# A hand-written order for the first batch's entry, an early activation table, filler matmuls, and later LoRA loads

## The chip, the cores and the metric

The kernel runs on one core of one Trainium2 chip. The metric is the device time of one execution in microseconds (us), taken as the median of several runs. Engines are named as in the profile: PE multiplies matrices into PSUM, DVE is the vector engine, ACT the scalar engine, POOL the third elementwise engine, SP issues most DMA transfers. [...]

## The reference

Two batches of 1024 tokens, 2048 features each. The first step normalises x per token, quantises it and a 2048 x 2048 context to 8 bits and adds their product to x; the second adds a 2048 x 2048 linear layer with a gated and a shared LoRA.

```python
def fake_quant(x, scale, zp):
    q = jnp.clip(jnp.round(x / s + z), 0.0, 255.0)
    return (q - z) * s
x = x + matmul(fake_quant(layernorm(x)), fake_quant(ctx))
h = layernorm(x)
x = x + h @ kernel + bias + (h @ A_eff.T) @ B_eff.T + (h @ A_shared.T) @ B_shared.T
```

## The kernel before

**Tiles.** A batch is 8 token tiles m of 128 rows (`prep_x`), two to a group g (4 groups, `y[g]`). The context is cut into 4 blocks n of 512 columns; a block comes in 8 loads of 256 rows (0.5 MB each). A *pair* (n, g) is the product of block n with group g: 2 x 16 matmuls of 128x128 by 128x512 (`xattn_pair`, line 367).

**One context load** (`quantise`): ACT scales and rounds it to int16 (line 318), DVE clips it, takes 128 off and writes bf16 (line 321). Three int16 buffers (`q2b`) lie between the two. Ten buffers (`lit`) take the loads; a load is issued when the one that used its buffer before has been rounded.

**One token tile** (`prep_x`): four `bn_stats` on DVE (283), their sum (257), the root on ACT (261), five small DVE steps to scale and offset (263 to 291), the row written as bytes by DVE (297), then for each half of the row: bytes less 128 to bf16 on ACT (302), 8 transposes on PE (307) and a copy out of PSUM by DVE (308). The sums give `r_s` (311, 312), the token's correction.

**One pair.** ACT writes column correction plus token correction into PSUM (365), PE adds the 16 products, DVE scales the result into y (381) and takes the statistics for the second normalisation (383). The column correction (`column_term`) is 16 narrow matmuls (337), a DVE copy (347), one matmul (349) and a DVE step (352). The very first pair has no column correction yet and gets both corrections from DVE afterwards (379). Pairs take three PSUM tiles in turn.

**Blocks 2 and 3** use the buffers of blocks 0 and 1, so block 2 can be written only when the last pair of block 0 has been multiplied. Between their loads come the LoRA A steps (`lora_a_step`: 394, 406, 414, 417), which need the gate matrix `gmat`, built at the start (236 to 248, 713).

**What sets the order.** A planner orders each engine's instructions by its own costs and priorities; `tc.high_priority` moves some ahead, `issue_after` keeps some back. None of them is written out by hand in the first batch.

**After the four blocks** come the second normalisation (439 to 450), `lora_ax` (459, copied out by ACT at 467), and the linear layer as a two-level fast product (630, 648), with `Delta` adding the LoRA part: each step loads a piece of `bd` and of the bias on ACT's queue (488, 489). In the second batch the entry is mixed into the first batch's linear layer.

Of the kernel before, what the change touches and what calls it, by code (L numbers as in the profile page):

```python
# [10 lines left out]
F32 = mybir.dt.float32  # L11
BF16 = mybir.dt.bfloat16
U8 = mybir.dt.uint8
# [53 lines left out]
def tile_quant_xattn_then_lora_ffn(  # L67
# [119 lines left out]


    sc = const.tile([P, 4], F32, tag="sc", name="sc")
    for i, s in enumerate((x1_scale, x1_zp, x2_scale, x2_zp)):  # L190
        (nc.sync, nc.scalar)[i % 2].dma_start(out=sc[:, i : i + 1], in_=s.partition_broadcast(P))
    load_x(0, 0)
    ahead[0] = 2
    load_next()
    load_x(0, 1)
    ahead[0] = 9
    load_next()
    load_x(0, 2)
    load_x(0, 3)

# [28 lines left out]
    for tag in ("acc0", "acc1", "delta"):  # L229
# [3 lines left out]


    m_ad = const.tile([P, NL], F32, tag="m_ad", name="m_ad")
    nc.vector.tensor_reduce(m_ad, ident.rearrange("p (n r) -> p n r", r=RC), AX.X, ALU.add)
    m_rk = const.tile([P, RC], F32, tag="m_rk", name="m_rk")
    nc.vector.tensor_reduce(m_rk, ident.rearrange("p (n r) -> p r n", r=RC), AX.X, ALU.add)
    gate_b = const.tile([P, GB, NL], F32, tag="gate_b", name="gate_b")
    nc.scalar.dma_start(  # L240
        out=gate_b.rearrange("p b n -> p (b n)"),
        in_=gate.rearrange("b n -> (b n)").partition_broadcast(P),
    )
    gval = const.tile([P, GB], F32, tag="gval", name="gval")
    nc.vector.tensor_tensor(gate_b, gate_b, m_ad.unsqueeze(1).to_broadcast([P, GB, NL]), ALU.mult)
    for b in range(B):
        for i in range(2):
            nc.vector.tensor_reduce(
                gval[:, ds(b * GPB + i * 2, 2)], gate_b[:, b * GPB + i : (b + 1) * GPB : 2, :], AX.X, ALU.add
            )  # L250

    def norm_stats(stats, name):
# [4 lines left out]
        nc.vector.tensor_scalar_add(ve, mv[:, 1:2], EPS)  # L259
        sd = small.tile([P, 1], F32, tag="sd", name=f"sd_{name}")  # L260
        nc.scalar.activation(sd, ve, AF.Sqrt)
        r0 = small.tile([P, 1], F32, tag="r0", name=f"r0_{name}")
        nc.vector.reciprocal(r0, sd)

        t = small.tile([P, 1], F32, tag="nt", name=f"nt_{name}")
        nc.vector.scalar_tensor_tensor(t, ve, r0, r0, ALU.mult, ALU.mult)
        nc.vector.tensor_scalar(t, t, -0.5, 1.5, ALU.mult, ALU.add)
        rstd = small.tile([P, 1], F32, tag="rstd", name=f"rstd_{name}")
        nc.vector.tensor_mul(rstd, r0, t)
        return mv[:, 0:1], rstd  # L270
# [5 lines left out]

    def prep_x(b, m, c1T, wk):

        nm = f"{b}_{m}"
        g, tok = m // MG, ds((m % MG) * P, P)  # L280
        ym = y[g][:, m % MG, :]
        for n in range(NN):
            nc.vector.bn_stats(st1[:, m, n, :], ym[:, ds(n * NB, NB)])  # L283
        with tc.high_priority() if b == 0 else nullcontext():
            mean, rstd = norm_stats(st1[:, m], f"a{nm}")

            k = small.tile([P, 1], F32, tag="kx", name=f"kx_{nm}")
            nc.vector.tensor_mul(k, rstd, inv1)
            o = small.tile([P, 1], F32, tag="ox", name=f"ox_{nm}")
            nc.vector.tensor_mul(o, mean, k)  # L290
            nc.vector.tensor_sub(o, z1, o)

            wf = flat(wk)
            q8 = wf[:, ds((m % 2) * (D // 4), D // 4)].bitcast(U8)
            qh = wf[:, D // 2 : D].bitcast(BF16)
            if b == 0:
                nc.vector.tensor_scalar(q8, ym, k, o, ALU.mult, ALU.add)
            else:
                nc.scalar.activation(q8, ym, AF.Identity, bias=o, scale=k)
        rsum = small.tile([P, 2], F32, tag="rsum", name=f"rsum_{nm}")  # L300
        for h in range(2):
            nc.scalar.activation(  # L302
# [3 lines left out]
            for kt in range(KH):  # L306
                nc.tensor.transpose(pt[:, kt, :], qh[:, ds(h * H + kt * P, P)], ident_h)  # L307
# [620 lines left out]
```

## Time and profile before

| what | value |
|---|---|
| median of 3 runs (lowest, highest) | 1118.43 us (1118.21, 1119.88) |
| the profiled execution, whole | 1118.22 us |
| its span of instructions | 1116.4 us |
| PE busy | 1070.9 us, 96% of the span |
| DVE, ACT, POOL busy | 752.5, 244.8, 262.2 us |
| PE's granted clock, mean of the execution | 0.994 |
| HBM traffic | 235 GB/s over the span |

Durations come from this one execution. Its whole time is 1.8 us more than its span, and 0.2 us less than the median. In a line of the timeline the columns are start, duration, engine, line, operation, output<-inputs, shape and count, and in brackets how long the engine sat idle before and what ended it. In a line of the stretches: the stretch, its length, busy time and number of instructions for each engine, the granted PE clock (1.00 is full), the busy share of the DMA engines and GB/s.

### The profile page before, as it was taken

To read this page: it belongs to the slowest core of one execution; us is meant where nothing else is said; L and a number is where in the kernel's file an instruction comes from. 1 tells how busy PE (TensorE), PEld (TensorE's weight loads), DVE (VectorE), ACT (ScalarE), POOL (GpSimd) and SP (SyncE) were. 2 spreads that over 40 slices of the span, in tenths; PEclk is the share of its full clock that TensorE was granted. 3 is DMA by queue.
4 is the path that set the end of the run, shared out by engine and by line. 5 is a ranking of instruction groups with operands and counts; after the bars stand their busy time and mean duration, and the time that the engine had idled before them with its cause. 6 is when DMAs were issued, how large, how long until landed. Compare 5 with 4: busy or idle time off the path is not lost.

```text
span 1116.4 us, 10654 instructions
## 1 busy us (share of the span) xinstructions
PE 1070.9 (96%) x3930; PEld 494.4 (44%) x3930; DVE 752.5 (67%) x979; ACT 244.8 (22%) x348; POOL 262.2 (23%) x106
## 2 busy tenths in 40 slices
PE   2699999999999999999999999999999999999998
PEld 1244435554444444444444433455444444444443
DVE  5895557566696677568768554766569686865851
ACT  4754414220000000001375651232000000000000
POOL 0000000234345413434000000022435343152600
PEclk9799999999999999999999999999999999999999
DMA  7982936887679746599866094588768874748511
GB/s 302 394 248 74 284 137 228 285 296 254 242 269 382 280 168 237 174 335 312 289 186 210 13 289 137 195 299 313 254 227 288 307 259 177 254 146 318 207 38 56
DMA packets 120772, 261.35 MB, mean 234 GB/s; under 512 B 11920, under 2 KB 16144, under 8 KB 119568
## 3 DMA queue, kind: packets, MB, share of 16 engines
q1 hardware_dynamic: 99264, 218.65, 56.7%
q10 hardware_dynamic: 21456, 42.02, 11.0%
q8 instruction: 31, 0.51, 0.2%
q14 instruction: 21, 0.17, 0.0%
HBM read 224.99 MB, written 37.75 MB: 235 GB/s over the span
## 4 chain that ended last, share of the span: by engine, by line
PE 81%; DVE 8%; DMA 6%; ACT 4%; issue 1%; SPq 0%; ACTq 0%; DVEq 0%
PE fu L630 33%; PE fv L630 17%; PE pa L367 12%; PE fw L630 9%; PE pl L502 3%; PE ptz L443 2%; DMA lit<-in_ctx_dram 2%; DVE st L283 2%; DMA zs<-lit 1%; PE px L459 1%; ACT big L302 1%; DMA lit<-in_lora_a_dram 1%; PE pg_b L394 1%; ACT q2b L318 1%; DMA bd<-q2b 1%
## 5 line engine op out<-in xcount | busy, mean ns | idle before, releaser
L630 PE MATMUL fu<-big,lit 128*128 128x512 f32 x896 | 395.3, 593 | 0.0
L579 POOL TENSOR_TENSOR lit<-lit,lit 128x1024 f32<-128x1024 f32 x56 | 162.4, 2908 | 523.9 <-DMA zs<-lit 202.0
L630 PEld LDWEIGHTS fu<-big,lit 128*128 128x128 f32 x896 | 168.7, 190 | 206.2 <-issue 204.9
L367 PE MATMUL pa<-big,big 128*128 128x512 bf16 x1024 | 239.4, 384 | 6.8 <-DVE big L321 3.9
L630 PE MATMUL fv<-big,lit 128*128 128x512 f32 x448 | 198.1, 594 | 0.0
L570 POOL TENSOR_TENSOR lit<-lit,lit 128x1024 f32<-128x1024 f32 x40 | 99.3, 2482 | 292.8 <-DMA lit<-zs 252.0
L579 DVE TENSOR_TENSOR big<-big,big 128x2048 f32<-128x2048 f32 x56 | 159.0, 2843 | 5.7 <-PE ptz L443 5.1
L367 PEld LDWEIGHTS <-big 128*128 128x128 bf16 x1024 | 97.7, 99 | 142.1 <-issue 39.8
L648 DVE TENSOR_TENSOR y<-y,fu 128x1024 f32<-128x1024 f32 (+1 forms) x98 | 113.7, 1194 | 66.1 <-PE fu L630 65.8
L630 PEld LDWEIGHTS fv<-big,lit 128*128 128x128 f32 x448 | 84.3, 190 | 105.0 <-issue 104.7
L648 DVE TENSOR_TENSOR y<-y,fv 128x1024 f32<-128x1024 f32 x48 | 56.8, 1218 | 89.2 <-PE fv L630 89.2
L318 ACT ACTIVATE q2b<-lit,sc,inv 128x1024 int16<-128x1024 f32 x64 | 76.6, 1230 | 156.9 <-DMA lit<-in_ctx_dram 140.5
L570 DVE TENSOR_TENSOR big<-big,big 128x2048 f32<-128x2048 f32 x40 | 101.2, 2529 | 10.9 <-DMA big<-in_w_dram 7.1
L630 PE MATMUL fw<-big,lit 128*128 128x512 f32 x224 | 99.1, 592 | 0.0
L381 DVE SCALAR_TENSOR_TENSOR y<-pa,k_s,y 128x1024 f32<-128x1024 f32 x32 | 41.0, 1281 | 62.2 <-PE pa L367 62.2
L491 ACT COPY pl<-bias 128x1024 f32<-128x1024 f32 x16 | 16.3, 1018 | 293.8 <-DVE y L513 281.2
L365 ACT ACTIVATE pa<-bp,r_s 128x512 f32<-128x512 f32 x62 | 41.4, 684 | 114.0 <-PE pa L367 65.3
L630 PEld LDWEIGHTS fw<-big,lit 128*128 128x128 f32 x224 | 42.2, 190 | 51.8 <-issue 51.8
L648 DVE TENSOR_TENSOR y<-y,fw 128x1024 f32<-128x1024 f32 x24 | 28.4, 1217 | 50.5 <-PE fw L630 50.5
L307 PE MATMUL pt<-ident_h,big 128*128 128x128 bf16 x256 | 20.4, 231 | 26.6 <-ACT big L302 26.2
L283 DVE BATCH_NORM_STATS2 st<-y 128x6 f32<-128x512 f32 x64 | 41.9, 681 | 2.2 <-DMA y<-in_x_dram 2.2
L321 DVE TENSOR_SCALAR big<-q2b 128x1024 bf16<-128x1024 int16 x64 | 27.4, 438 | 22.3 <-ACT q2b L318 18.5
(84 smaller groups left out, 625.2 us busy)
## 6 DMA issues: line engine op xcount, KB each, us to landing
big<-in_w_dram SPq DMA_DIRECT2D x96, 1024.0 KB
lit<-zs SPq DMA_DIRECT2D x88, 512.0 KB
lit<-in_ctx_dram SPq DMA_DIRECT2D x64, 512.0 KB
out_dram<-y ACTq DMA_DIRECT2D x30, 512.0 KB
zs<-lit ACTq DMA_DIRECT2D x24, 512.0 KB
y<-in_x_dram SPq DMA_DIRECT2D x8, 1024.0 KB
lit<-in_lora_a_dram SPq DMA_DIRECT2D x32, 256.0 KB
lit<-in_lora_bt_dram SPq DMA_DIRECT2D x32, 256.0 KB
```

Of the source, the lines that this page charges most:

```text
L283: nc.vector.bn_stats(st1[:, m, n, :], ym[:, ds(n * NB, NB)])
L318: nc.scalar.activation(qi, t, AF.Relu, bias=z2, scale=inv2)
L321: nc.vector.tensor_scalar(c2[r // 4][:, ds(2 * (r % 4), 2), :], qi, QMAX, CENTRE, ALU.min, ALU.subtract)
L365: nc.scalar.activation(pa[:, j, :], colt[n], AF.Identity, bias=r_s[:, m : m + 1])
L367: nc.tensor.matmul(pa[:, j, :], c1T[g][:, k, ds(j * P, P)], c2[k // 8][:, k % 8, :], start=(first_product and k == 0), stop=(k == KT - 1), ...
L381: summed = nc.vector.scalar_tensor_tensor(yp, pa, s12, yp, ALU.mult, ALU.add)
L443: nc.tensor.transpose(pt[:, k, :], t[:, ds((4 * u + k) * P, P)], ident)
L502: nc.tensor.matmul(pl[j][i][:, half], axT[rows, pr, ds(j * P, P)], bt[rows, half], start=False, stop=True, skip_group_check=True,)
L570: line(eng.tensor_tensor(got[0], got[0], got[1], ALU.add if terms[1][2] > 0 else ALU.subtract))
L579: line(eng.tensor_tensor(out_t, at[p], at[q], op))
L630: nc.tensor.matmul(ps[:, m, :], at[:, k, ds(m * P, P)], bt[:, k, :], start=(opens and k == 0), stop=(ends and k == KQ - 1), skip_group_che ...
L648: line(nc.vector.tensor_tensor(yp, yp, chains[chain][:, js, :], ALU.add if sign > 0 else ALU.subtract))
```

## The change

For the first batch only, a function `entry` writes out every step of blocks 0 and 1 and of all eight token tiles; `in_order` ties the instructions of DVE, ACT and PE to that order. The work is the same but for this:

- A root of a constant (`warm`) runs on ACT at the start, so the table for the root is loaded there.
- The first context load comes alone ahead of the second token tile.
- The gate values are loaded and reduced after the entry and not at the start.
- Scale and offset take five DVE steps with none for the plain reciprocal deviation (two fewer for a row written by DVE, one fewer for one by ACT), and `r_s` takes one instruction for two. This holds in both batches.
- In tiles 4, 5 and 6 the row of bytes is written by ACT, not DVE; in tiles 4 to 7 the second half's copy out of PSUM is ACT's.
- The pairs (0, 0) and (1, 0) begin without corrections and get them from DVE (`late`).
- Filler matmuls (`keep_busy`): 8 behind the first root, 14 behind the first column correction. Nothing reads them.
- The `bn_stats` of the eight pairs come after the entry; their DVE scaling stays in it but for the last two.
- Work on block 2 is kept back behind the entry's last ACT instruction in the planned order; before, three of its roundings ran in between.
- In both batches the loads of `bd` and bias in `Delta` are kept back behind the copy at the end of the first `lora_ax`.

```diff
+    last_of = {}
+    @contextmanager
+    def in_order(*engines):
+        traced = nc.cur_bb.bb.instructions
+        last = traced[-1]
+        yield
+        start = next(k for k in reversed(range(len(traced))) if traced[k] is last) + 1
+        for i in list(traced[start:]):
+            if i.engine in engines:
+                if i.engine in last_of:
+                    tc.add_manual_dep(
+                        i,
+                        last_of[i.engine].name,
+                        mybir.DependencyInfo(mybir.DependencyClass.NoSync, mybir.DependencyReason.DATA),
+                        reason="in_order",
+                    )
+                last_of[i.engine] = i
     sc = const.tile([P, 4], F32, tag="sc", name="sc")
     for i, s in enumerate((x1_scale, x1_zp, x2_scale, x2_zp)):
         (nc.sync, nc.scalar)[i % 2].dma_start(out=sc[:, i : i + 1], in_=s.partition_broadcast(P))
+    warm = const.tile([P, 1], F32, tag="warm", name="warm")
+    nc.gpsimd.memset(warm, 1.0)
+    nc.scalar.activation(warm, warm, AF.Sqrt)
     load_x(0, 0)
-    ahead[0] = 2
+    ahead[0] = 1
     load_next()
     load_x(0, 1)
-    ahead[0] = 9
+    ahead[0] = 8
     load_next()
     load_x(0, 2)
     load_x(0, 3)
+    ahead[0] = 9
...
+    def gate_values():
...
+    class XTile:
+        def __init__(self, b, m, c1T, wk):
...
+            self.on_vector = b == 0 and m not in (4, 5, 6)
+            self.q8 = wf[:, ds((m % 2) * (D // 4), D // 4)].bitcast(U8)
...
+        def stats(self, *ns):
+            for n in ns:
+                nc.vector.bn_stats(st1[:, self.m, n, :], self.y[:, ds(n * NB, NB)])
+        def root(self):
+            self.root_d()
+            self.root_a()
+        def root_d(self):
+            self.mean, self.ve = variance(st1[:, self.m], f"a{self.nm}")
+        def root_a(self):
+            self.sd = root_of(self.ve, f"a{self.nm}")
+        def factors(self):
+            r0, t = end_norm(self.ve, self.sd, f"a{self.nm}")
+            self.k = small.tile([P, 1], F32, tag="kx", name=f"kx_{self.nm}")
+            nc.vector.scalar_tensor_tensor(self.k, r0, t, inv1, ALU.mult, ALU.mult)
+            self.o = small.tile([P, 1], F32, tag="ox", name=f"ox_{self.nm}")
+            if self.on_vector:
+                nc.vector.scalar_tensor_tensor(self.o, self.mean, self.k, z1, ALU.mult, ALU.subtract)
+            else:
+                nc.vector.tensor_mul(self.o, self.mean, self.k)
+                nc.vector.tensor_sub(self.o, z1, self.o)
+        def row(self):
+            if self.on_vector:
+                nc.vector.tensor_scalar(self.q8, self.y, self.k, self.o, ALU.mult, ALU.subtract)
+            else:
+                nc.scalar.activation(self.q8, self.y, AF.Identity, bias=self.o, scale=self.k)
+            self.rsum = small.tile([P, 2], F32, tag="rsum", name=f"rsum_{self.nm}")
+        def centre(self, h):
+            nc.scalar.activation(
+                self.qh[:, ds(h * H, H)],
+                self.q8[:, ds(h * H, H)],
+                AF.Identity,
+                bias=n_centre,
+                accum_out=self.rsum[:, h : h + 1],
+            )
...
+        def place(self, h):
+            if self.b == 0 and self.m >= 4 and h == 1:
+                return nc.scalar.copy(self.to[h], self.pt[h])
+            return nc.vector.tensor_copy(self.to[h], self.pt[h])
+        def total(self):
+            nc.vector.tensor_scalar(
+                r_s[:, self.m : self.m + 1], self.rsum[:, 0:1], self.rsum[:, 1:2], d2, ALU.add, ALU.mult
+            )
...
+        def begin(self, j):
+            m = self.g * MG + j
+            nc.scalar.activation(self.pa[:, j, :], colt[self.n], AF.Identity, bias=r_s[:, m : m + 1])
+        def late(self, j):
+            m, pj = self.g * MG + j, self.pa[:, j, :]
+            nc.vector.scalar_tensor_tensor(pj, colt[self.n], r_s[:, m : m + 1], pj, ALU.add, ALU.add)
+        def end(self):
+            yp = y[self.g][:, :, ds(self.n * NB, NB)]
+            return nc.vector.scalar_tensor_tensor(yp, self.pa, s12, yp, ALU.mult, ALU.add)
...
+        def __init__(self, b, behind):
+            self.b, self.behind = b, behind
...
-            nc.scalar.dma_start(out=bt, in_=bd[self.b][ds(2 * pr, 2), :, :, cols].rearrange("g s r n -> (g s r) n"))
-            nc.scalar.dma_start(out=bb, in_=bias[cols].partition_broadcast(P))
+            with tc.issue_after(self.behind):
+                nc.scalar.dma_start(
+                    out=bt, in_=bd[self.b][ds(2 * pr, 2), :, :, cols].rearrange("g s r n -> (g s r) n")
+                )
+                nc.scalar.dma_start(out=bb, in_=bias[cols].partition_broadcast(P))
...
+    def entry():
+        X = [XTile(0, m, c1T, wk) for m in range(MT)]
+        qi = {}
+        def rounded(*rs):
+            for r in rs:
+                qi[r] = round_ctx()
+        def centred(*rs):
+            for r in rs:
+                centre_ctx(c2[r // NR], r % NR, qi.pop(r))
+        def slices(pair, j, *rs):
+            for r in rs:
+                pair.products(j, range(2 * r, 2 * r + 2), begun=False)
+        def keep_busy(n):
+            for i in range(n):
+                nc.tensor.matmul(idle[:, i % 2, :], ones_h, tick.to_broadcast([P, NB]), start=True, stop=True)
+        idle = ps_acc.tile([P, 2, NB], F32, tag="delta", name="idle")
+        tick = const.tile([P, 1], BF16, tag="tick", name="tick")
+        X[0].stats(0, 1, 2, 3)
+        X[0].root()
+        nc.scalar.activation(tick, ident_h[:, 0:1], AF.Identity, scale=X[0].ve)
+        keep_busy(8)
+        X[0].factors()
+        X[0].row()
+        rounded(0)
+        for h in range(2):
+            X[0].centre(h)
+            X[0].turn(h)
+        centred(0)
+        X[1].stats(0, 1)
+        X[0].place(0)
+        X[1].stats(2)
+        X[0].place(1)
+        X[1].stats(3)
+        A = Pair(0, 0, 0, c1T, c2[0])
+        slices(A, 0, 0)
+        rounded(1, 2)
+        X[1].root()
+        centred(1)
+        slices(A, 0, 1)
+        rounded(3, 4)
+        X[1].factors()
+        X[1].row()
+        centred(2, 3, 4)
+        X[1].centre(0)
+        slices(A, 0, 2, 3)
+        X[1].turn(0)
+        X[1].place(0)
+        X[1].centre(1)
+        X[1].turn(1)
+        X[1].place(1)
+        X[0].total()
+        X[1].total()
+        slices(A, 0, 4)
+        slices(A, 1, 0, 1, 2, 3, 4)
+        rounded(5, 6)
+        for m in range(4, MT):
+            load_x(0, m)
+        centred(5)
+        slices(A, 0, 5)
+        slices(A, 1, 5)
+        X[2].stats(0)
+        rounded(7)
+        centred(6)
+        slices(A, 0, 6)
+        slices(A, 1, 6)
+        X[2].stats(1)
+        centred(7)
+        slices(A, 0, 7)
+        slices(A, 1, 7)
+        X[2].stats(2, 3)
+        parts = column_parts(0, 0, c2[0])
+        X[2].root_d()
+        rounded(8)
+        X[2].root_a()
+        rounded(9)
+        column_end(0, 0, parts)
+        keep_busy(14)
+        X[2].factors()
+        X[2].row()
+        rounded(10)
+        for h in range(2):
+            X[2].centre(h)
+            X[2].turn(h)
+        centred(8, 9)
+        X[3].stats(0)
+        centred(10)
+        X[2].place(0)
+        X[3].stats(1)
+        X[2].total()
+        X[2].place(1)
+        C = Pair(0, 0, 1, c1T, c2[0])
+        F = Pair(0, 1, 0, c1T, c2[1])
+        rounded(11)
+        C.begin(0)
+        C.products(0, range(KT))
+        X[3].stats(2, 3)
+        X[3].root()
+        centred(11)
+        slices(F, 0, 0, 1, 2, 3)
+        rounded(12, 13)
+        X[3].factors()
+        X[3].row()
+        X[3].centre(0)
+        centred(12, 13)
+        slices(F, 0, 4, 5)
+        X[3].turn(0)
+        X[3].centre(1)
+        X[3].turn(1)
+        X[3].place(0)
+        X[3].total()
+        X[3].place(1)
+        C.begin(1)
+        C.products(1, range(KT))
+        rounded(14, 15)
+        for j in range(MG):
+            A.late(j)
+        centred(14, 15)
+        A.end()
+        X[4].stats(0)
+        parts = column_parts(0, 1, c2[1])
+        slices(F, 0, 6, 7)
+        X[4].stats(1)
+        column_end(0, 1, parts)
+        F.products(1, range(KT), begun=False)
+        G = Pair(0, 1, 1, c1T, c2[1])
+        for j in range(MG):
+            G.begin(j)
+        X[4].stats(2, 3)
+        X[4].root()
+        C.end()
+        X[4].factors()
+        X[4].row()
+        G.products(0, range(KT))
+        G.products(1, range(KH))
+        for h in range(2):
+            X[4].centre(h)
+            X[4].turn(h)
+        G.products(1, range(KH, KT))
+        for j in range(MG):
+            F.late(j)
+        X[5].stats(0, 1, 2, 3)
+        X[4].place(0)
+        X[4].total()
+        X[4].place(1)
+        H = Pair(0, 0, 2, c1T, c2[0])
+        H.begin(0)
+        H.products(0, range(KT))
+        X[5].root()
+        F.end()
+        I = Pair(0, 1, 2, c1T, c2[1])
+        X[5].factors()
+        X[5].row()
+        I.begin(0)
+        G.end()
+        I.products(0, range(10))
+        X[5].centre(0)
+        X[5].turn(0)
+        I.products(0, range(10, KT))
+        X[5].centre(1)
+        X[5].turn(1)
+        X[6].stats(0, 1, 2, 3)
+        X[5].place(0)
+        X[5].total()
+        X[6].root()
+        X[5].place(1)
+        for p in (H, I):
+            p.begin(1)
+        H.products(1, range(KT))
+        X[6].factors()
+        X[6].row()
+        X[7].stats(0, 1, 2, 3)
+        X[7].root_d()
+        H.end()
+        I.products(1, range(4))
+        X[6].centre(0)
+        X[6].turn(0)
+        I.products(1, range(4, 10))
+        X[6].centre(1)
+        X[6].turn(1)
+        I.products(1, range(10, KT))
+        X[7].root_a()
+        X[6].place(0)
+        X[6].total()
+        X[6].place(1)
+        J = Pair(0, 0, 3, c1T, c2[0])
+        J.begin(0)
+        J.products(0, range(12))
+        X[7].factors()
+        X[7].row()
+        I.end()
+        X[7].centre(0)
+        X[7].turn(0)
+        J.products(0, range(12, KT))
+        X[7].centre(1)
+        X[7].turn(1)
+        K = Pair(0, 1, 3, c1T, c2[1])
+        K.begin(0)
+        K.products(0, range(6))
+        opened = X[7].place(0)
+        X[7].total()
+        X[7].place(1)
+        for p in (J, K):
+            p.begin(1)
+        J.products(1, range(KT))
+        K.products(0, range(6, KT))
+        K.products(1, range(KT))
+        return opened, (A, C, F, G, H, I, J, K)
+    def next_block(b, n):
+        close_c2(n)
+        open_c2(n + 2)
+        bp.give(colt.pop(n))
+        if n == 0:
+            for r in range(NR):
+                quantise(c2[2], r)
+                if r % 4 == 3:
+                    lora_a_step(b, r // 4)
+            column_term(b, 2, c2[2])
+    opened = None
+    for b in range(B):
         if b == 0:
             open_c2(0)
-            prep_x(0, 0, c1T, wk)
-            for r in range(NR):
-                quantise(c2[0], r)
-                if r == 3:
-                    prep_x(0, 1, c1T, wk)
-            for m in range(4, MT):
-                load_x(0, m)
             open_c2(1)
-        opened = xattn_pair(b, 0, 0, c1T, c2[0], first_product=(b == 0))
-        if b == 0:
-            for r in range(4):
-                quantise(c2[1], r)
-            for m in (2, 3):
-                prep_x(b, m, c1T, wk)
-        xattn_pair(b, 0, 1, c1T, c2[0])
-        if b == 0:
-            for r in range(4, NR):
-                quantise(c2[1], r)
-            column_term(b, 1, c2[1])
-        for g in range(2):
-            xattn_pair(b, 1, g, c1T, c2[1])
-        for g in range(2, GPB):
-            for m in range(g * MG, (g + 1) * MG):
-                with tc.issue_after(opened.ins):
-                    prep_x(b, m, c1T, wk)
-            for n in range(2):
-                xattn_pair(b, n, g, c1T, c2[n])
-                if g + 1 == GPB:
-                    close_c2(n)
-                    open_c2(n + 2)
-                    bp.give(colt.pop(n))
-                    if n == 0:
-                        for r in range(NR):
-                            quantise(c2[2], r)
-                            if r % 4 == 3:
-                                lora_a_step(b, r // 4)
-                        column_term(b, 2, c2[2])
+            with in_order(mybir.EngineType.DVE, mybir.EngineType.Activation, mybir.EngineType.PE):
+                opened, begun = entry()
+            with tc.issue_after(opened.ins), tc.issue_after(last_of[mybir.EngineType.Activation]):
+                begun[6].end()
+                gate_values()
+                gate_matrix(0)
+                next_block(b, 0)
+                begun[7].end()
+                next_block(b, 1)
+                for p in begun:
+                    p.stats()
+        else:
...
-                lora_ax(b, 0, [zqs[0], zqs[1]])
+                ax = lora_ax(b, 0, [zqs[0], zqs[1]])
...
-        ffn(b, first, meanwhile)
+        ffn(b, first, ax.ins, meanwhile)
```

## Prediction

> **What bounds the kernel now.** I read the page's busy times first (PE 1070.9 of 1116.4 us), then its slices, to see where the missing 45 us lie, then stretches of the trace cut at the events of the first batch.
>
> ```profile
> PE   2699999999999999999999999999999999999998
> PEclk9799999999999999999999999999999999999999
> ```
>
> A slice is 28 us: PE idles in the first two and hardly anywhere else. The stretches (columns as in the section above; DMA share 1 is full):
>
> ```profile
> 0.00:44.00 44.00, 17.35 (x88) 7.32 (x88) 28.11 (x83) 22.38 (x26) 1.26 (x10) 0.96 0.89 337
> 44.00:60.00 16.00, 10.94 (x66) 5.37 (x67) 14.95 (x41) 11.11 (x17) 0.00 (x0) 0.68 1.04 357
> 60.00:90.00 30.00, 29.57 (x160) 14.18 (x159) 25.37 (x66) 15.12 (x25) 0.00 (x0) 1.00 0.68 194
> 90.00:117.15 27.15, 26.07 (x158) 11.66 (x157) 18.36 (x39) 16.27 (x19) 0.00 (x0) 1.00 0.45 137
> 117.15:127.80 10.65, 10.57 (x51) 4.54 (x51) 5.60 (x9) 6.53 (x8) 0.00 (x0) 1.00 1.05 310
> 187.65:238.00 50.35, 48.24 (x293) 29.09 (x291) 32.28 (x52) 15.95 (x33) 10.60 (x5) 1.00 0.82 291
> 238.00:538.00 300.00, 300.00 (x777) 135.93 (x777) 213.98 (x146) 18.98 (x25) 117.64 (x43) 1.00 0.76 270
> ```
>
> Up to 60 us PE loses 31.7 us; from 60 to 187.65 only 1.7; then 2.1, of which 1.25 is one gap before line 443; then nothing for 300 us. So after 60 us time is gained only by giving PE its remaining work earlier. Between 40 and 54 us two things meet: little to multiply, and a slow clock.
>
> ```profile
> 37.91 1.12 PE L349 MATMUL pc<-q2b,mean_w 128*128 128x512 f32 x2 [0.79 <-DVE q2b L347]
> 44.41 2.17 PE L307 MATMUL pt<-ident_h,big 128*128 128x128 bf16 x16 [5.37 <-ACT big L302]
> 49.50 5.96 PE L367 MATMUL pa<-big,big 128*128 128x512 bf16 x16 [2.93 <-DVE big L321]
> ```
> ```profile
> 44.00:50.00 6.00, 2.56 (x18) 1.87 (x19) 5.88 (x15) 6.00 (x9) 0.00 (x0) 0.50 1.02 426
> 50.00:54.00 4.00, 4.00 (x11) 1.35 (x10) 3.10 (x10) 1.99 (x4) 0.00 (x0) 0.50 1.01 383
> 54.00:58.00 4.00, 3.50 (x38) 1.75 (x36) 3.96 (x10) 2.42 (x5) 0.00 (x0) 0.96 1.07 272
> ```
>
> PE waits 5.37 us for tile 2 and 2.93 for the next context piece, and its first eleven products after 49.5 take 0.427 us each instead of 0.2155.
>
> I name the pairs in entry order: A (0,0), C (0,1), F (1,0), G (1,1), then H, I, J, K. The end of K and the start of pair (2,0) are what the rest of the kernel hangs on. Before, both are at 117.15 (59 products in a row; 11 are K's):
>
> ```profile
> 114.68 13.14 PE L367 MATMUL pa<-big,big 128*128 128x512 bf16 x59
> ```
>
> **The change.** I take the planned order of each engine and start each instruction when its engine is free and its inputs are there, with durations of the trace; the results are estimates. Used: `bn_stats` 0.60, row on DVE 1.35, on ACT 2.10 (second batch), two centre halves 2.4, rounding 1.15, eight transposes 0.45, column term 1.05 + 1.12, line 381 1.20, a small DVE step 0.2, a hand-over between engines 0.04 to 0.1.
>
> *Table and X0.* The rows of ACT:
>
> ```profile
> 13.39 1.28 ACT L318 ACT_TABLE_LOAD   x1 [13.39 <-DMA lit<-in_ctx_dram]
> 14.69 1.24 ACT L318 ACTIVATE q2b<-lit,sc,inv 128x1024 int16<-128x1024 f32 x1
> 15.95 1.28 ACT L261 ACT_TABLE_LOAD   x1
> 17.24 0.20 ACT L261 ACTIVATE sd_a<-ve_a 128x1 f32<-128x1 f32 x1
> ```
>
> `warm` loads the root's table while ACT waits for data; the first load of all falls away. The first root need not follow a rounding and a load. [...] With x0 landing at about 9.3 and no gate reductions, X0's row is written at about 15.05 (before: 20.49), A's last product ends at 34.1 (36.8).
>
> *Filler.* Eight matmuls at half clock (3.4 us) end before X0's transposes can start; fourteen at full clock (3.0) fill the wait for tile 2. Their cover is PE's idleness; if X0 or X2 were ready at once, they would cost these 6.4 us.
>
> *Tile 2.* A end 34.1, narrow matmuls 35.15, DVE copy 35.9, mean matmul 37.05, correction 37.9, factors 38.95, row 40.3, centres 42.7, rounding (11) 43.8, C begins about 44.5: 5.0 us before 49.50. The context loads (one per 1.35 us, the last of block 1 landing near 40) and x4 to x7 (42.7 to 50.2) come in time.
>
> *Clock.* Entered as 0. The row: in before the clock fell 1.6 us after PE's last product, in a window one third busy. A fall like it costs ten products x 0.211 = 2.1 us. [...] Both bounds go into the range.
>
> *C to K.* From 44.55 PE has 224 products x 0.2155 = 48.3, five tiles' transposes 4.5, a column term 2.1: 54.9 us. But DVE and ACT are now in written order, and for tiles 4 to 6 one tile's round on ACT (row 2.1, centres 2.4, waits for a turn queued behind six products, copy, two begins 1.3) comes to about 9.6 us, against 7.8 of PE work. PE idles about 6.1, and K ends at 105.55. The copy of 1024 PSUM elements by ACT isn't in the trace: between 0.59 (512 elements) and 1.30 (two of line 365); I take 1.05 (line 491 has 1024 f32 in 1.018). Per tile that is -0.45 to +0.25.
>
> *Behind K.* 11.6 us of gain, then, and most of it is given back. Before, block 2 was partly loaded under the entry; now its roundings stand behind the entry's last ACT instruction, and DVE has J's and K's scaling, the block's clips and 16 deferred `bn_stats` (9.6 us) in one queue. The first LoRA steps (three of pg_a and pga 4.9, column term 2.15: 7.05 us) stand on PE before pair (2,0), whose begin on ACT stands behind the roundings, and round 6 waits for a buffer that a late pga step frees. The gate DMA, issued near 97, is wanted near 99.75: its landing costs 0 to 5. By my table pair (2,0) starts at 118.1: 105.55 + 7.05 + 5.5 of waiting. Before, 117.15 plus 1.65 for a pg_a and a pga that now come earlier is 118.8 for equal work. The gain is **0.7**.
>
> *Delta.* In both batches line 488 stands ahead of the copy of `axT`:
>
> ```profile
> 205.31 0.33 ACTq L488 DMA_DIRECT2D bp<-bd  x1
> 205.68 0.37 ACT L467 COPY axT<-px 128x256 f32<-128x256 f32 x1 [10.61 <-DMA big<-in_w_dram]
> 206.11 0.66 PE L443 MATMUL ptz<-ident,big 128*128 128x128 f32 x4 [1.25 <-ACT axT L467]
> ```
> ```profile
> 742.16 0.33 ACTq L488 DMA_DIRECT2D bp<-bd  x1
> 742.53 0.37 ACT L467 COPY axT<-px 128x256 f32<-128x256 f32 x1 [10.57 <-DMA bd<-q2b]
> 742.96 0.66 PE L443 MATMUL ptz<-ident,big 128*128 128x128 f32 x4 [1.21 <-ACT axT L467]
> ```
>
> The issue waits for a free `bp` buffer, the copy waits behind it, and PE for the copy. Moved behind, the gaps go: 1.25 + 1.21 = **2.46** (bounds 0 to 3.4, all idleness of PE near there). `bd` is wanted only when the first product chain ends, so its later start is covered.
>
> *Second batch.* A tile has two DVE steps fewer; eight tiles mixed into work where PE idles 1.2 us (600 to 630): about **0.3**.
>
> Sum on the profiled execution: 1118.22 - 0.7 - 2.46 - 0.3 = 1114.76. The median lies 0.2 above it: **1115.0**. 0.2% is 2.24 us, about what can be told from no change.
>
> **Rivals.**
> - *The tail is hidden* (0.2). If scalings, clips and LoRA copies get through in time, pair (2,0) starts at 105.55 + 7.05 = 112.6: 6.2 us instead of 0.7, **1109.5**. For: DVE is busy 18.4 of 27 us before, and the statistics may be planned last. Against: roundings, begins and clips share two ordered queues.
> - *Slower: the written round of tiles 4 to 7 on ACT is longer* (0.3). It has about eight hand-overs per tile; I charge under 0.1 for each. At 1.3 us more per round over five rounds, pair (2,0) comes 6.5 later: **1121.5**. It breaks even at 0.7 per round (3.46 / 5) and is measurably slower from 1.14 ((3.46 + 2.24) / 5). For: PE idles only 1.5 us from 60 to 117 today, with the planner free to move work; a fixed order can't. Against: the durations are measured.
> - *The entry does nothing*, since loads set it (inside the main case): only Delta and the second batch remain, 1118.43 - 2.76 = 1115.7. Against: X0 waits for ACT, not for loads, up to 17.24.
>
> **How the numbers follow.** Main case 0.5: own range 1111.5 (gate in time, cheap copy) to 1118.5 (a clock fall of 2.1 and 1.4 in rounds). Hidden tail 0.2: 1105 to 1111.5. Slower rounds 0.3: 1118 to 1124. Leaving out a tenth at each end gives 1108 to 1121.5. Faster than 1116.19: 0.19 of the hidden tail, 0.34 of the main case, 0.53. Slower than 1120.67: 0.18 of the rounds, 0.05 for a late gate or clock falls in the main case: 0.23. Same: 0.24.
>
> **What would show it.** C starts near 44.5 at full clock; K ends near 105.5; PE then waits about 5.5 us before pair (2,0) near 118; the gaps before line 467's readers near 206 and 743 are gone; no table load after 10 us. I am wrong if rounds of tiles 4 to 7 take over 10.7 us, if pair (2,0) starts before 115, if the half clock returns after 30 us, or if PE finds a new gap where `bd` is first used.

## The result and the profile after

The changed kernel takes 1126.43 us (median of 5 runs, 1121.70 to 1129.25); the kernel before took 1118.21 us beside it (1117.89 to 1119.88). The ratio is 1.0065 (95% interval 1.0046 to 1.0084): slower by 8.2 us, where 1115.0 was forecast. The runs also lie 7.6 us apart, those of before 2.0. The profiled execution of after took 1128.38 us, with a span of 1126.6.

The slices of the page (after, 28 us each):

```profile
PE   4888899899999999999999999989999999999998
PEclk7899999899999999999999999999999999999999
```

PE is busier in the first two slices than before (4 and 8 tenths against 2 and 6), as it should be. But the third to the fifth, full before, have holes. The stretches cut at the same times as before (stretch, length, busy time and count of PE, weight loads, DVE, ACT, POOL, then the granted clock, DMA share, GB/s):

```profile
0.00:44.00 44.00, 24.99 (x124) 11.37 (x127) 26.96 (x67) 23.70 (x31) 1.29 (x11) 0.79 0.90 347
44.00:60.00 16.00, 14.52 (x78) 6.41 (x79) 10.85 (x24) 7.90 (x11) 0.00 (x0) 0.84 1.04 339
60.00:90.00 30.00, 27.15 (x156) 13.45 (x157) 24.04 (x59) 19.64 (x27) 0.00 (x0) 1.00 0.44 125
90.00:117.15 27.15, 23.15 (x127) 9.79 (x126) 22.94 (x52) 18.54 (x20) 0.00 (x0) 0.88 0.57 178
187.65:238.00 50.35, 45.70 (x250) 26.68 (x251) 26.07 (x55) 15.97 (x33) 10.16 (x4) 0.93 0.73 257
```

From 60 to 90 us PE loses 2.9 us (0.4 before), from 90 to 117.15 it loses 4.0 (1.1), from 187.65 to 238 it loses 4.7 (2.1); and the clock is below full in the fourth and the fifth line, where it was full before.

The entry itself came out nearly as planned. The chain before C in PE's timeline (start, duration, line, what ended the idle time before):

```profile
35.49 1.10 PE L450 MATMUL pc<-q2b,mean_w 128*128 128x512 f32 x2 [0.89 <-DVE q2b L444]
36.42 3.21 PE L861 MATMUL idle<-tick,ones_h 128*128 128x512 bf16 x13
41.17 0.62 PE L375 MATMUL pt<-ident_h,big 128*128 128x128 bf16 x8 [1.54 <-ACT big L364]
42.30 1.03 PE L375 MATMUL pt<-ident_h,big 128*128 128x128 bf16 x8 [0.51 <-ACT big L364]
44.13 8.58 PE L471 MATMUL pa<-big,big 128*128 128x512 bf16 x28 [0.79 <-ACT pa L467]
```

C begins at 44.13 (forecast 44.5, before 49.50). But its 28 products take 8.58 us, and 6.20 at full clock in e2_bias_early: the clock fell at 42.15, in the second of the two waits for tile 2 (1.54 and 0.51 us), and it fell twice more later in this execution (at 110.42 and 216.23). The granted clock (the last figure but two of each line) in stretches of 4 us, with stretches left out at the ... lines:

```profile
38.00:42.00 4.00, 2.19 (x15) 0.98 (x14) 3.54 (x8) 2.32 (x4) 0.00 (x0) 1.00 1.02 417
42.00:46.00 4.00, 2.90 (x13) 1.58 (x14) 3.85 (x9) 2.29 (x6) 0.00 (x0) 0.52 1.01 420
...
110.00:114.00 4.00, 2.86 (x12) 0.82 (x12) 3.34 (x10) 2.48 (x2) 0.00 (x0) 0.55 1.05 395
114.00:118.00 4.00, 2.97 (x21) 1.25 (x21) 2.69 (x8) 1.43 (x2) 0.00 (x0) 0.59 1.07 283
...
216.00:220.00 4.00, 2.53 (x9) 2.10 (x10) 0.73 (x1) 3.01 (x5) 0.00 (x0) 0.53 0.45 178
```

K ends at 107.21 and pair (2,0) begins at 123.97, 16.8 us later (forecast 105.55, 118.1):

```profile
107.21 1.07 PE L513 MATMUL pg_a<-lit,gmat 128*32 128x512 f32 x8
123.97 6.29 PE L471 MATMUL pa<-big,big 128*128 128x512 bf16 x27
```

The Delta edit did remove the gap it was aimed at, and made a larger one a few us on. ACT's timeline in the first batch (ACTq is a DMA issue, ... marks lines left out):

```profile
207.06 0.37 ACT L586 COPY axT<-px 128x256 f32<-128x256 f32 x1 [7.99 <-PE px L578]
207.20 0.33 ACTq L608 DMA_DIRECT2D bp<-bd  x1
207.56 0.50 ACTq L611 DMA_DIRECT2D bias<-in_bias_dram  x1
...
215.89 1.02 ACT L613 COPY pl<-bias 128x1024 f32<-128x1024 f32 x1 [4.62 <-DMA bias<-in_bias_dram]
216.84 1.06 ACT L563 COPY lit<-ptz 128x512 f32<-128x512 f32 x2
```

and PE's behind it:

```profile
217.47 1.97 PE L562 MATMUL ptz<-ident,big 128*128 128x128 f32 x8 [4.29 <-ACT lit L563]
219.23 5.50 PE L752 MATMUL fu<-big,lit 128*128 128x512 f32 x8
```

The bias, held back together with `bd`, is issued at 207.56 and read by an ACT copy at 215.89. That copy stands ahead of the copies out of PSUM (563), and PE waits 4.29 us for those; the clock falls to half within this gap, at 216.23, and the next eight fp32 products take 5.50 us (3.60 at full clock, in e2_bias_early). The second batch has the same gap, there without a fall of the clock (1.00 from 750 to 764 us):

```profile
757.28 1.14 PE L562 MATMUL ptz<-ident,big 128*128 128x128 f32 x8 [2.97 <-ACT lit L563]
```

To see where the 10.2 us of span were lost I compare two events of each batch: the first `px` product (before Delta) and the first `fw` product (behind its first step).

| stage, us | before | after |
|---|---|---|
| start to first px | 195.89 | 199.88 (+4.0) |
| px to fw, first batch | 19.63 | 24.69 (+5.1) |
| fw to second batch's px | 517.26 | 516.44 (-0.8) |
| px to fw, second batch | 18.98 | 20.69 (+1.7) |
| from there to the end | 364.67 | 364.87 (+0.2) |

So in this execution there are two questions: 6.8 us around the Delta edit, 4.0 in the entry.

### The profile page after: what moved, and what is told of

Same layout as the page of the kernel before. It is cut to its first block, busy times and chain, and to the rows that moved or that the text cites. A ratio compares the mean times of both kernels' runs of the same rounds, so it can differ in the third digit from the quotient of the medians.

```text
span 1126.6 us, 10630 instructions
## 1 busy us (share of the span) xinstructions
PE 1079.7 (96%) x3919; PEld 499.1 (44%) x3952; DVE 749.3 (67%) x937; ACT 253.5 (23%) x354; POOL 261.8 (23%) x107
## 4 chain that ended last, share of the span: by engine, by line
PE 83%; DVE 6%; DMA 5%; ACT 3%; issue 2%; SPq 0%; DVEq 0%; ACTq 0%
PE fu L752 33%; PE fv L752 17%; PE pa L471 13%; PE fw L752 9%; PE pl L624 3%; PE ptz L562 2%; PE px L578 2%; DVE st L332 1%; DMA bias<-in_bias_dram 1%; DMA bd<-q2b 1%; PE pt L375 1%; DVE st L491 1%; PE pg_b L513 1%; PE pg_a L513 1%; DMA big<-in_w_dram 1%
## 5 line engine op out<-in xcount | busy, mean ns | idle before, releaser
L471 PE MATMUL pa<-big,big 128*128 128x512 bf16 x992 | 235.2, 384 | 12.0 <-ACT pa L467 6.0
L613 ACT COPY pl<-bias 128x1024 f32<-128x1024 f32 x16 | 16.3, 1017 | 302.0 <-DVE y L635 281.6
L562 PE MATMUL ptz<-ident,big 128*128 128x128 f32 x256 | 36.0, 282 | 7.8 <-ACT lit L563 7.7
L635 DVE TENSOR_TENSOR y<-pl,y 128x512 f32<-128x512 f32 x64 | 40.0, 680 | 1.5 <-PE pl L624 0.8
```

What stands on the lines that cost most here:

```text
L471: nc.tensor.matmul(self.pa[:, j, :], self.c1T[:, k, ds(j * P, P)], self.c2[k // 8][:, k % 8, :], start=(not begun and k == 0), stop=(k == ...
L562: nc.tensor.transpose(pt[:, k, :], t[:, ds((4 * u + k) * P, P)], ident)
L635: line(nc.vector.tensor_add(yb, pl[j][i], yb))
```

## The experiments

Theory 1, for Delta, is that the bias load is the new wait; its rival is that those gaps come from the moved entry. Theory C, for the entry, is the clock; theory Q is DVE's queue behind K; rival L is late loads behind K.

**Delta.** Four runs, undoing or doing that edit on either kernel.

e1_loads_back: the changed kernel with both loads in their old place.

```diff
-            with tc.issue_after(self.behind):
-                nc.scalar.dma_start(out=bt, in_=bd[self.b][ds(2 * pr, 2), :, :, cols].rearrange("g s r n -> (g s r) n"))
-                nc.scalar.dma_start(out=bb, in_=bias[cols].partition_broadcast(P))
+            nc.scalar.dma_start(out=bt, in_=bd[self.b][ds(2 * pr, 2), :, :, cols].rearrange("g s r n -> (g s r) n"))
+            nc.scalar.dma_start(out=bb, in_=bias[cols].partition_broadcast(P))
```

> The changed kernel with the loads of bd and bias in Delta put back ahead of the copy of axT, as in the kernel before; nothing else. Theory 1 (the bias load, held back with bd, lands late, the ACT copy that reads it stands ahead of the copies out of PSUM, and PE waits 4.3 and 3.0 us and loses its clock once): about 1126.4 less 5 for the first batch and 1 for the second, 1120 to 1121. Rival (those gaps come from the later entry and have nothing to do with Delta): 1126, with gaps of 3 to 4 us still near 213 and 754.

1123.21 us (1120.11 to 1124.38), 3.2 below the changed kernel. The gaps of 4.29 and 2.97 us are gone, an old one (1.34 us at 212.23) is back. The direction is that of theory 1, but 6 us were expected and 3.2 came. The two profiles tell why for their two executions: the two stages from px to fw shrink by 5.2 and 1.8 us, as expected, but 0.7 us comes back between them, and the entry of this execution ended 2.1 us later. The run also bears on the other question: with Delta's loads in their old place the kernel is still 4.6 us slower than before (ratio 1.0037, 1.0023 to 1.0050), so the entry by itself is slower too.

e2_bias_early: the changed kernel with only `bd` held back.

```diff
+            nc.scalar.dma_start(out=bb, in_=bias[cols].partition_broadcast(P))
             with tc.issue_after(self.behind):
                 nc.scalar.dma_start(out=bt, in_=bd[self.b][ds(2 * pr, 2), :, :, cols].rearrange("g s r n -> (g s r) n"))
-                nc.scalar.dma_start(out=bb, in_=bias[cols].partition_broadcast(P))
```

> The changed kernel with only the load of bd held back, the bias load in its old place. Theory 1: both the old gaps (1.25 and 1.21 us) and the new ones (4.3 and 3.0) are gone, so 1 to 2.5 us below the run with both loads put back: 1118 to 1120. Rival (bd is what lands late): like the changed kernel, 1125 to 1127.

1118.99 us (1114.71 to 1122.30, 13 runs): as expected, 7.4 below the changed kernel and level with before (ratio 0.9996, 0.9984 to 1.0008).

e3_before_held: the kernel before with both loads held back, the change's edit alone.

> The kernel before with one edit of the change, both Delta loads held back behind the copy of axT. Theory 1: slower than before by the two new gaps less the two old ones, 4.3 + 3.0 - 2.5 = 4.8, with 0 to 2 more for the clock: 1122 to 1125. The prediction's step: 1118.2 - 2.46 = 1115.8.

1120.76 us, ratio 1.0021 (1.0012 to 1.0030): slower by 2.2. The direction of theory 1, below its range. The prediction's 1115.8 falls, and so does the rival: the edit alone makes the gap in the old entry too. PE's timeline of this run:

```profile
211.22 1.15 PE L443 MATMUL ptz<-ident,big 128*128 128x128 f32 x8 [2.73 <-ACT lit L444]
```

It is 2.73 us here and not 4.29, because the bias landed 6.8 us after its issue (202.87 to the copy at 209.64) and not 8.3; and the clock did not fall there (the eight fp32 products behind it take 3.60 us).

e4_before_bias_early: the kernel before with only `bd` held back.

> The kernel before with only the load of bd held back behind the copy of axT. Theory 1 with nothing else in the way: 1115.8 (both old gaps of 1.2 us gone). Rival: bd itself is written only by 205.3 and 742.2 in the kernel before, and its load now stands ahead of the next copies out of PSUM, so the gap moves from one copy to the next and the time is that of before, 1117.5 to 1118.5.

1116.04 us, ratio 0.9975 (0.9964 to 0.9985): 2.5 faster, the prediction's 2.46. That they agree so well is in part luck, for ACT's timeline shows that the rival is half right:

```profile
204.24 0.37 ACT L467 COPY axT<-px 128x256 f32<-128x256 f32 x1 [7.99 <-PE px L459]
204.38 3.02 ACTq L490 DMA_DIRECT2D bp<-bd  x2
207.44 1.08 ACT L444 COPY lit<-ptz 128x512 f32<-128x512 f32 x2 [2.83 <-DMA big<-in_w_dram]
```

`axT` is copied at once, the issue of `bd` then holds ACT's queue for 3.02 us, and the next copies wait behind it: PE has a gap of 1.18 us in place of 1.25, and 0.30 in place of 1.21 in the second batch. From px to fw the profiles differ by 0.56 and 0.77 us, 1.3 in all. The linear layers give 1.3 and 0.8 us more, in stretches in which PE's idle time did not shrink, and the entry of this execution ended 1.2 us later; where these come from stays open.

**The entry.** The base is now e2_bias_early (1119.0), 3.0 us above e4, which has the old entry. Its profile caught an execution (1116.13 us, mean clock 0.998) in which C's 28 products took 6.20 us, and the clock read 1.00 from 74 to 130 us, though the waits near tile 2 are those of the changed kernel and one of them is longer:

```profile
40.73 0.62 PE L375 MATMUL pt<-ident_h,big 128*128 128x128 bf16 x8 [1.54 <-ACT big L364]
41.86 0.62 PE L375 MATMUL pt<-ident_h,big 128*128 128x128 bf16 x8 [0.51 <-ACT big L364]
43.69 6.20 PE L471 MATMUL pa<-big,big 128*128 128x512 bf16 x28 [1.21 <-ACT pa L467]
```

K ends at 104.40, and then

```profile
104.40 1.06 PE L513 MATMUL pg_a<-lit,gmat 128*32 128x512 f32 x8
107.49 0.63 PE L533 MATMUL pga<-ident,q2b 128*128 128x128 f32 x4 [2.03 <-DVE q2b L525]
108.05 1.06 PE L513 MATMUL pg_a<-lit,gmat 128*32 128x512 f32 x8
110.60 0.63 PE L533 MATMUL pga<-ident,q2b 128*128 128x128 f32 x4 [1.49 <-DVE q2b L525]
111.16 1.05 PE L434 MATMUL pcp<-big,ones_h 128*32 128x512 bf16 x16
113.09 1.10 PE L450 MATMUL pc<-q2b,mean_w 128*128 128x512 f32 x2 [0.89 <-DVE q2b L444]
115.89 3.82 PE L513 MATMUL pg_a<-lit,gmat 128*32 128x512 f32 x8 [1.70 <-issue]
120.58 0.63 PE L533 MATMUL pga<-ident,q2b 128*128 128x128 f32 x4 [0.88 <-ACT pa L467]
121.05 9.30 PE L471 MATMUL pa<-big,big 128*128 128x512 bf16 x41
```

16.65 us, of which some 6.9 are work: 2.03 + 1.49 + 0.89 behind DVE's queue, 1.70 and 2.8 more within the third LoRA step (8 products that take 1.06 elsewhere take 3.82), and 0.88. The profile names no releaser for the 1.70; SP issues that step's loads at 109.42, after the second step's products have freed buffers.

e5_stats_late: the 16 deferred statistics kept back behind the scaling of pair (2,0).

```diff
-                for p in begun:
-                    p.stats()
...
-            xattn_pair(b, 2, g, c1T, c2[2])
+            opened = xattn_pair(b, 2, g, c1T, c2[2])
+            if b == 0 and g == 0:
+                with tc.issue_after(opened.ins):
+                    for p in begun:
+                        p.stats()
```

> The kernel of e2_bias_early (1119.0) with the 16 deferred bn_stats of the eight pairs kept back behind the scaling of pair (2,0). Theory Q (behind K the LoRA and column copies stand behind statistics in DVE's queue; PE waits 2.0 + 1.5 + 0.9 us for them): 3 to 5 us faster, 1114 to 1116. Rival L (the loads that come late at 115.9 set the start of pair (2,0)): 0 to 1 us faster, 1118 to 1119, with the wait moved to the third LoRA step.

1117.09 us (ratio to before 0.9980, 0.9969 to 0.9991): 1.9 faster than e2_bias_early, between the two, though the two intervals overlap. The first wait shrank from 2.03 to 1.07 us, but PE now stands longer at the third step's loads (2.10 us, then 3.95 for the products).

e6_free_rounding: block 2's work no longer tied to the entry's last ACT instruction.

```diff
-            with tc.issue_after(opened.ins), tc.issue_after(last_of[mybir.EngineType.Activation]):
+            with tc.issue_after(opened.ins):
```

> The kernel of e2_bias_early (1119.0) without the tie of block 2's work to the entry's last ACT instruction; it may stand anywhere behind X7's first placing in the plan's own order. Rival L (no context buffer is freed from 74 to 98 us, the DMA engines stand still, and the loads behind K come late): 3 to 4 us faster, 1115 to 1116. Theory Q (DVE's queue sets the stretch behind K): within 1 us, 1118 to 1120. Third: the roundings lie in the way of tiles 6 and 7 on ACT and K ends later, 1120 to 1122.

1116.15 us (ratio 0.9976, 0.9965 to 0.9986): 2.8 faster, a little less than rival L expected. Three roundings of block 2 now run inside the entry, the first at 60.99 us, and the buffers that they free let SP issue a LoRA step's four loads at 62.24 us, which left at 96.98 in e2_bias_early. Most of the standstill stays: from 82 to 98 us the DMA engines move 1 GB/s here, 5 in e2_bias_early, 9 in the kernel before. And the third LoRA step still waits for its load (1.81 us, then 2.75 for the products). So the tie costs some 2.8 us; how much of that is the earlier loads and how much the three roundings that no longer stand behind K isn't shown. The statistics cost some 1.9; neither is the whole.

e7_no_filler: both `keep_busy` calls removed.

> The kernel of e2_bias_early (1119.0) without its 22 filler matmuls. Theory C (how long PE was idle in the last few us sets the clock, and the filler holds it): C starts at the same time but always at half clock, A too: 2 to 5 us slower, 1121 to 1124, spread smaller. Rival (the clock falls by chance whatever stands there, or the filler is in the way): 1118 to 1119.

1121.13 us (1118.43 to 1125.13, 18 runs): 2.1 slower, with a mean clock of 0.984 to 0.992 in every run; the spread, 6.7 us, is hardly smaller. PE idles 4.59 us before tile 2, and the clock is below full in C: 26 of its products take 7.36 us, where e2's profile has 28 in 6.20. The change's filler was worth its place.

e8_more_filler: more of it, around tile 2 (as in e9) and in the waits behind K.

> The kernel of e2_bias_early (1119.0) with more filler where PE waits: 20 instead of 14 behind the first column correction, 2 behind each half turn of X2, and 17 in the waits behind K (8 and 7 behind the first two LoRA products, 2 ahead of them). Theory C (each fall of the clock follows gaps of 1.2 to 2 us and costs some 3 us): falls behind 30 us become rare; 1115 to 1117 and a spread under 4 us instead of 7.6. Rival (the spread has another cause): 1119 to 1121, spread as before.

1118.09 us (1116.42 to 1120.96): spread 4.5 us instead of 7.6 (the width expected was under 4), all 13 runs at a mean clock of 0.993 or more; but 0.9 us faster only, and so out of both ranges expected. The start of pair (2,0), behind late loads, came no earlier: 16.5 us after K.

e9_fill_x2: more filler around tile 2 alone.

```diff
-        keep_busy(14)
+        keep_busy(20)
...
         for h in range(2):
             X[2].centre(h)
             X[2].turn(h)
+            keep_busy(2)
```

> The kernel of e2_bias_early (1119.0) with more filler around tile 2 alone (20 instead of 14 behind the first column correction, 2 behind each half turn of X2); nothing added behind K. Theory C with the fall near 42 us as the usual one: the mean clock stays at 0.993 or more in most runs, 1116 to 1118, spread 5 or less. Rival (the filler behind K did it in e8): as e2_bias_early, 1118.5 to 1119.5, most runs at a mean clock of 0.988 to 0.991.

1116.26 us (1115.64 to 1118.56, 13 runs; ratio 0.9986, 0.9978 to 0.9994), a mean clock of 0.992 or more in every run. The first of tile 2's waits is 0.23 us and not 1.54, and C's 28 products take 6.20 us, as in e2's profile:

```profile
42.22 0.62 PE L375 MATMUL pt<-ident_h,big 128*128 128x128 bf16 x8 [0.23 <-ACT big L364]
45.18 6.20 PE L471 MATMUL pa<-big,big 128*128 128x512 bf16 x28 [0.78 <-ACT pa L467]
```

In e2_bias_early 8 of 13 runs had 0.988 to 0.991, with times of 1117.9 to 1122.3; the other five took 1114.7 to 1116.1. So theory C holds: filling the waits of tile 2 is worth 2.7 us in the median and takes away most of the spread. That each of the eight fell near 42 us isn't shown: from 0.998 to 0.989 is some 20 us at half clock (an estimate: 0.009 of 1116 us, twice), and the fall there lasts 6.83 us in the profile of after, so there were others too. What remains of the entry is 1116.26 against 1116.04 (e4), within the noise nothing.

e10_late_free: e5 and e6 together.

> The kernel of e2_bias_early (1119.0) with both the late statistics of e5 (-1.9) and the untied roundings of e6 (-2.8). Two separate waits: 1114.3. The same wait, met from two sides: 1115.5 to 1116.5.

1114.23 us (1109.69 to 1116.65, 8 runs; ratio 0.9958, 0.9943 to 0.9973): the sum of the two gains. That it fits to a tenth is luck, with an interval of 1.7 us either way; the other expectation, 1115.5 or more, lies just outside it. Runs of like clock say the same: at a mean clock of 0.996 or more e2, e5, e6 and e10 took 1115.8, 1112.8, 1113.0 and 1110.3 us (medians of 4, 3, 2 and 1 runs). So they are two separate waits, as far as these runs can tell.

e11_late_free_fill: e10 with the filler of e9.

> The kernel of e10_late_free with the filler of e9_fill_x2 around tile 2. Theory C: 1 to 2 us below e10_late_free, 1112.5 to 1114, few runs under a mean clock of 0.993. Rival (the filler only delays C): as e10_late_free or up to 1 us slower.

1111.23 us (1110.49 to 1111.98), ratio 0.9937 (0.9925 to 0.9949): 7.1 us faster than before, 15 below the changed kernel, and the five runs agree within 1.5 us. That is 3.0 below e10_late_free, more than the 1 to 2 expected. It holds every idea of the change but the place of the bias load, the tie and the place of the statistics. Behind K:

```profile
115.42 2.09 PE L513 MATMUL pg_a<-lit,gmat 128*32 128x512 f32 x8 [0.56 <-DMA lit<-in_lora_a_dram]
117.44 10.53 PE L471 MATMUL pa<-big,big 128*128 128x512 bf16 x48
```

e12_lora_after: e11 with the third LoRA step on PE behind pair (2,0).

```diff
-                lora_a_step(b, g + 1)
+                with tc.issue_after(pair20.ins) if b == 0 and g == 1 else nullcontext():
+                    lora_a_step(b, g + 1)
```

Here `pair20` is the last product of pair (2,0) on PE.

> The kernel of e11_late_free_fill with the third LoRA A step queued on PE behind pair (2,0) instead of ahead of it. Rival L (that step's load comes late and PE stands still for it, 1.8 us and more): 1.5 to 3 us below e11_late_free_fill, 1110 to 1112.5. Otherwise (the begin of pair (2,0), behind the roundings and the column correction, is as late): as e11_late_free_fill.

1114.06 us, 2.8 slower than e11: outside both expectations.

```profile
113.46 1.10 PE L451 MATMUL pc<-q2b,mean_w 128*128 128x512 f32 x2 [0.89 <-DVE q2b L445]
116.68 12.21 PE L472 MATMUL pa<-big,big 128*128 128x512 bf16 x48 [2.12 <-ACT pa L468]
```

With the step gone PE waits for the begin on ACT instead, which is as late as before (115.96 against 116.26), and in this execution the 48 products take 12.21 us and not 10.53, at a mean clock of 0.990 (0.996 in e11's). That in e11 the step, waiting for its own load, did the filler's work is a guess. At the first px product the two profiles are 2.05 us apart; another 0.9 is a wait for DVE ahead of `fw`. The clock need not be the cause in the other runs: the five have mean clocks of 0.990 and 0.995 (0.996 to 0.997 in e11), and those at 0.995 are no faster (1113.7 to 1114.5 us) than those at 0.990 (1113.7 and 1114.1). What makes up the 2.8 us stays open in part.

## Why the prediction was wrong, point by point

Three steps failed. In the Delta edit the later loads were taken as covered, and the bias load was not: a gain of 2.46 us was forecast, a loss of 3.2 came. The clock was entered as 0, and its fall near tile 2 is worth 2.7. The waits behind K were put at 5.5 us and are 9.8.

- *Table and X0, tile 2*: right. The table is loaded at 1.66, X0's row starts at 14.95 and ends at 16.3 (15.05 for its end was 1.2 early), A ends at 33.6 (34.1), C begins at 44.13 (44.5). The instruction behind the table load starts 0.02 us after its end (1.66 + 1.28 is 2.94, and it starts at 2.96); in before it was 0.01 (15.95 + 1.28 is 17.23, and 17.24).
- *Rounds of tiles 4 to 7*: right. The rows on ACT start at 66.33, 74.57 and 83.98, rounds of 8.2 and 9.4 us (9.6). The copy out of PSUM takes 1.01 (1.05). The slower rival named this place, and it did not happen; the kernel got slower elsewhere.
- *Gate DMA*: issued at 97.70, its product on DVE starts at 101.45 without waiting. It cost 0, the lower bound.
- *Clock, entered as 0*: a failed step. No run shows this term: in the profile of after the clock fell at 42.15 us, where the longest gap is 1.54 us, and filling these waits is worth 2.7 us in the median (e2 against e9), a little over the 2.1 taken from the row of before. The execution of e2's profile went without this fall (C's 28 products in 6.20 us).
- *Behind K*: the waits were put at 5.5 us and are 9.8 without any clock fall. The prediction had the DVE queue (4.4 measured), but no term for late loads: the third LoRA step's 4.5 us. The tie to ACT's last instruction, which also holds back the freeing of buffers, is a part of their cause only, for without it (e6) that step still loses 3.5.
- *Entry as a whole, -0.7*: as it was changed, +3.0 (e2 against e4) or +4.6 (e1 against before), so the wrong sign; with tile 2's waits filled, +0.2 (e9 against e4). That the last comes close is luck: in e2's profile K ended 1.15 us earlier than planned (104.40), and the waits behind it were 4.3 us longer.
- *Delta, -2.46*: the step that failed most, +3.2 on the changed kernel (after against e1) and +2.2 on the kernel before (e3). "`bd` is wanted only when the first product chain ends, so its later start is covered" holds for `bd`'s landing, though its issue then holds ACT's queue and leaves a gap of 1.18 us (e4). But the moved block issues two transfers, and the second one, the bias, is wanted by an ACT copy that stands ahead of the copies out of PSUM. The price of holding the bias back is 7.4 us on the changed kernel (after against e2) and 4.7 on the kernel before (e3 against e4): a landing time of 6.8 to 8.3 us, two gaps, and, on the changed kernel's profile, a fall of the clock. The idea without the bias brings 2.5 (e4) and, on the changed kernel, 4.2 (e2 against e1). The prediction counted a new gap near there among its signs of being wrong, but gave it no time.
- *Second batch, -0.3*: from fw to the second px it is 517.26 before and 517.16 in e1, so 0.1. (Before, a tile has seven small DVE steps from line 263 to 291, not five.)

From before to after in medians: the `bd` part -2.5 (e4), the entry +0.2 (e9), the clock at tile 2 +2.7 (e2), the bias +7.4, together +7.8 of the 8.2 measured. These are the steps of one chain of runs (before, e4, e9, e2, after), so their sum has to come out near 8.2 and proves nothing; in another order the shares differ, 4.6 for the entry (e1) and 3.2 for Delta. The range's upper end, 1121.5, was too low because no rival had a stall in the Delta edit and because the clock bound was used for one place only; in the profile of after it fell in three behind 30 us (42.15, 110.42, 216.23).

## What to carry to other kernels

When a block of issues is moved behind something, list every transfer in it and the first reader of each, and what stands behind that reader in its queue: the price of a late small load is paid there. A written order that ends in "everything else behind this" can also delay the freeing of buffers (four loads by 35 us here), so ask which loads those buffers would have started. And before a chain is shortened, look at how full PE is in the few us around it: in the profile of after the clock fell within gaps of 1.54 and 0.51 us and stayed at half for 6.83 us, and filling these gaps was worth 2.7 us in the median here (e2 against e9).

## What the runs showed of the hardware

The traces of before and after hold six whole stretches in which the granted clock reads 0.50 (a last one in each, cut off by the end of the trace, is left out). Four last 6.83 us, one 10.24 and one 13.65: 2, 3 and 4 times 3.41 us. In e6 the readings of 0.86 and 0.72 from 114 to 122 us come to 3.4 us at half clock. The table takes pieces of 3.41 us, the one that ends where the clock falls and those of the stretch at half clock, and gives the share of each in which PE was busy (weight loads not counted; an estimate, since the ends of matmuls are modelled):

| the clock falls at, us | half clock for, us | PE busy in the 3.41 us before | in the pieces at half clock |
|---|---|---|---|
| before 40.63 | 13.65 | 0.33 | 0.00, 0.61, 0.40, 1.00 |
| after 8.02 | 10.24 | 0.00 | 0.00, 0.25, 0.99 |
| after 21.67 | 6.83 | 0.42 | 0.41, 1.00 |
| after 42.15 | 6.83 | 0.44 | 0.72, 1.00 |
| after 110.42 | 6.83 | 0.41 | 0.80, 0.86 |
| after 216.23 | 6.83 | 0.11 | 0.64, 1.00 |

Before these six falls PE was busy for at most 0.44 of the piece; at half clock it was busy for 0.86 or more of each last piece and for 0.80 or less of those ahead of it. A low share alone doesn't tell: in before the clock reads 1.00 from 4 to 18 us, where PE did nothing, and in e2 from 106 to 110 us, where PE was busy for 1.62 of 4.00 us. Waits of 1.54 and 0.51 us near tile 2 went with a fall in the profile of after and without one in that of e2 (C's 28 products in 8.58 and 6.20 us). One and the same kernel ran from 1114.7 to 1122.3 us (e2), and 10 more filler matmuls brought it to 1115.6 to 1118.6 (e9); where the clock fell in the executions without a profile wasn't seen.
